# Turning attention values with shifted identities in SBUF, postponing the first adjacency pieces, and ending layer 0's norm on ScalarE

## The chip, the cores and the metric

The kernel runs on one core of one Trainium2 chip. The core has five engines with a queue of instructions each: TensorE (PE; its weight loads are shown apart as PEld), VectorE (DVE), ScalarE (ACT), GpSimd (POOL) and SyncE (SP), which only issues DMAs. Sixteen DMA engines move data between DRAM, where all inputs lie, and SBUF, the on-chip memory that the engines read; TensorE writes to PSUM, from where DVE or ACT copy results away. The metric is the device time of one execution in microseconds, given as the median of repeated runs.

## The reference

Four layers over 3327 nodes with 128 features, each followed by a residual and a layer norm. Layer 0 is attention with a weighted adjacency matrix as edge bias; layers 1 to 3 are graph convolutions with the same matrix:

```python
q = (x @ Wq.T).reshape(d, n, h)      # d = 128, n = 3327, h = 8
k = (x @ Wk.T).reshape(d, n, h)
v = (x @ Wv.T).reshape(d, n, h)
a = softmax(einsum('dnh,dmh->dnm', q, k) * scale + adj + adj, axis=2)
out = einsum('dnm,dmh->dnh', a, v).reshape(n, h * d)
x0 = layernorm(x + out @ Wo.T)
# layer 1: normalised (adj + I) @ (x @ W.T + b); layer 2: adj/deg and adj.T/deg;  layer 3: [x, adj @ x] @ W.T + b
```

The reshape is a plain reinterpretation of memory: the 3327 rows of 1024 projected numbers are read again as 128 "heads" of 3327 rows with 8 numbers. With one slot being 8 numbers, a row of the projection holds 128 slots, and head d begins at slot 3327 d, in the middle of a row. So a head's rows are not aligned to rows of x, and head d + 1 is shifted against head d.

## The kernel before

**Setup** (the block of pools at lines 241 to 378). x is read in seven super-blocks of 512 rows (`u`, the last one half as long), transposed on PE into `xT` (L267) and multiplied by the weights, which are transposed so that a column is (h, j) (`load_by_h`, L166). The products (`products`, L281) go through two PSUM buffers `pp`. Three things happen with them:

- For queries and keys (L324 to L336) ACT writes a rounded copy `hi` (L330), DVE the rest `lo` (L331) and the largest magnitude of `hi` (L333), and the POOL queue stores both to DRAM tensors of slots `q_s` and `k_s` (L275). `hi` and `lo` have two buffers each.
- For values (L284 to L288) the product is copied into `pv` and stored by the POOL queue to `vT_s` in DRAM (L275). `values_turned(g)` then reads sixteen heads of it back, shifted as the flat layout has it (`vt`, L300, on the SP queue), transposes 26 tiles of 128 tokens on PE (L312), copies them to `vo` (L317), and stores `vo` from the ACT queue to `v_img` (L320), the layout that attention reads.
- For the first super-block of 512 rows of the adjacency matrix (u = 0), thirteen "pieces" of 512 x 256 are loaded (`piece_load`, L185), transposed in 32 x 32 blocks, reduced for row maxima, row sums and column sums (`piece_work`, L200 to L216), and stored transposed to `adjT_s` in 16 small DMAs each on the POOL queue (`piece_store`, L224). Row maxima go to `lead_s` (L237).

Outside of `manual_schedule` a scheduler orders each engine's queue from the dependencies and its own estimates; the order is fixed when the kernel is compiled.

**Attention** (`attention`, from L381; the order is written out by hand). 28 blocks are worked through: seven chunks of 476 queries times four ranges of keys (`KBS`). In each block 32 groups of four heads are computed: scores on PE (L575), exponentials on ACT (L583; a few on DVE, L539 to L546), weighted values on PE (L600). DMAs of queries and keys are issued two groups ahead, the POOL copies values into padded tiles (L481). In every eighth group one more piece of the adjacency matrix is handled in the background (`background`, `background_work`); the list `pieces` has u = 1 to 6, 78 pieces, so it is used up after 624 of the 896 groups.

**After attention** (from L943). For each of 26 tiles of 128 nodes `divide` loads the attention output `o` (L1054, SP queue), takes a reciprocal on DVE (`rec`, L1056), multiplies on POOL (`on`, L1058); PE transposes (L1066), multiplies by Wo (L1075); DVE adds x (L1078) and `norm` ends with L1008 on DVE, `(h - mean) * rstd`. This is stage 0. Then come four passes over the stored adjacency matrix, in which PE works without gaps.

Of the kernel before, what the change touches and what calls it, by code (L numbers as in the profile page):

```python
# [19 lines left out]
P = 128  # L20
# [30 lines left out]
def kernel(ctx: ExitStack, tc: tile.TileContext, x, adj, wq, wk, wv, wo,  # L51
# [31 lines left out]
    def tokens(t):  # L83
        return P - 1 if t == T - 1 else P
# [31 lines left out]
    vT_s = scratch.tile([H, SLOTS], F32, name="vT_s")  # L116
# [78 lines left out]
    def piece_work(pool, u, c, ai):  # L195

        nj = PIECE // 32
        w = min(PIECE, N - c * PIECE)
        at = pool.tile([P, nj, 4, 32], F32, name="at")
        nc.vector.transpose(at.rearrange("p j t b -> p t j b"), ai.rearrange("p t (j a) -> p t j a", a=32))  # L200
        yield at
        if c == 0:
            maxima[u] = pool.tile([P, 4, NPC], F32, name="pmax")
            sums[u] = pool.tile([P, 4, NPC], F32, name="psum")
        nc.vector.tensor_reduce(maxima[u][:, :, c], ai[:, :, 0:w], AX.X, ALU.max)
        yield at
        nc.vector.tensor_reduce(sums[u][:, :, c], ai[:, :, 0:w], AX.X, ALU.add)
        yield at
        part = csum[:, c * nj:(c + 1) * nj]
        if u == 0:  # L210
            nc.vector.tensor_reduce(part, at.rearrange("p j t b -> p j (t b)"), AX.X, ALU.add)
        else:
            cs = pool.tile([P, nj], F32, name="cs")
            nc.vector.tensor_reduce(cs, at.rearrange("p j t b -> p j (t b)"), AX.X, ALU.add)
            nc.vector.tensor_tensor(part, part, cs, ALU.add)
        yield at  # L216

    def piece_store(pool, u, c, at):
# [8 lines left out]
        if c == NPC - 1:  # L227
            nc.vector.tensor_reduce(rsum[:, u, :], sums[u], AX.X, ALU.add)
            top = pool.tile([P, 4], F32, name="rtop")
            nc.vector.tensor_reduce(top, maxima[u], AX.X, ALU.max)  # L230
            hi = pool.tile([P, 4], F32R, name="rhi")
            nc.vector.tensor_copy(hi, top)
            lo = pool.tile([P, 4], F32R, name="rlo")
            nc.vector.tensor_tensor(lo, top, hi.bitcast(F32), ALU.subtract)
            for row, sb in enumerate((hi, lo)):
                for i in range(4):
                    nc.gpsimd.dma_start(out=flat_ap(lead_s[u], row * SUPER + i * P, [[1, 32], [32, 4]]),  # L237
                                        in_=sb[32 * i:32 * i + 32, :].bitcast(F32))


    with tc.tile_pool(name="pw", bufs=1) as pw, tc.tile_pool(name="pa", bufs=2) as pa, \
            tc.tile_pool(name="pe", bufs=2) as pe, \
# [10 lines left out]
        wvT = load_by_h(pw, ppw, wv, "wvT")  # L253
        for u in range(NU):
# [10 lines left out]
            ps = pps.tile([P, 4, P], F32, tag="ps", name="xtr")  # L265
            for r in range(R):
                nc.tensor.transpose(ps[:, r, :], xr[:, r, :], ident)  # L267
            copy(u, xT[:, u, 0:R, :], ps[:, 0:R, :])
# [14 lines left out]

        for u in range(NU):  # L284
            pv = pa.tile([P, H, 4, D], F32, tag="hi", name="pv")
            for r in range(spread(u)[1]):
                copy(u + r, pv[:, :, r, :], products(u, r, wvT))
            store_slots(nc.gpsimd, vT_s, 0, u, pv)  # L288

        wqT = load_by_h(pw, ppw, wq, "wqT")  # L290
        wkT = load_by_h(pw, ppw, wk, "wkT")
        top_q = pw.tile([P, NU, 4], F32, name="top_q")
        top_k = pw.tile([P, NU, 4], F32, name="top_k")
        nc.gpsimd.memset(top_q, 0.0)
        nc.gpsimd.memset(top_k, 0.0)

        def values_turned(g):

            vt = pa.tile([P, N], F32, name="vt")
            nc.sync.dma_start(out=vt, in_=flat_ap(vT_s, g * 16 * N, [[N, 16], [SLOTS, H], [1, N]]))  # L300
            vo = pa.tile([P, 4 * T * 32], F32, name="vo")

            nc.gpsimd.memset(vo[96:P, :], 0.0)
            i = 0
            for k0, nt in KBS:
                vb = vo[:, 4 * 32 * k0:4 * 32 * (k0 + nt)].rearrange("p (g s c) -> p s g c", g=4, c=32)
                for s0 in range(0, nt, 4):
                    ns = min(4, nt - s0)
                    ps = pps.tile([P, 4, P], F32, tag="ps", name="vtr")
                    for j in range(ns):  # L310
                        m = tokens(k0 + s0 + j)
                        nc.tensor.transpose(ps[:m, j, :], vt[:, (k0 + s0 + j) * P:(k0 + s0 + j) * P + m], ident)  # L312
                    m = tokens(k0 + s0 + ns - 1)
                    for b, e in ([(0, ns)] if m == P else [(0, ns - 1), (ns - 1, ns)]):
                        if b < e:
                            mm = tokens(k0 + s0 + e - 1)
                            copy(i, vb[:mm, s0 + b:s0 + e], ps[:mm, b:e, :].rearrange("p s (g c) -> p s g c", g=4))  # L317
                    i += 1
                w = nt * 32
                nc.scalar.dma_start(  # L320
                    out=flat_ap(v_img, k0 * HD + g * 4 * w, [[T * HD, P], [w, 4], [1, w]]),
                    in_=vo[:, 4 * 32 * k0:4 * 32 * (k0 + nt)].rearrange("p (g c) -> p g c", g=4))

        for u in range(NU):  # L324
            for w, s, top, f in ((wqT, q_s, top_q, SCALE / 2), (wkT, k_s, top_k, 1.0)):
                hi = pa.tile([P, H, 4, D], F32R, tag="hi", name="hi")
                lo = pa.tile([P, H, 4, D], F32R, tag="lo", name="lo")
                for r in range(spread(u)[1]):
                    pp = products(u, r, w)
                    nc.scalar.activation(hi[:, :, r, :], pp, AF.Copy, scale=f)  # L330
                    nc.vector.scalar_tensor_tensor(lo[:, :, r, :], pp, f, hi[:, :, r, :].bitcast(F32),  # L331
                                                   ALU.mult, ALU.subtract)
                    nc.vector.tensor_reduce(top[:, u, r:r + 1], hi[:, :, r, :].bitcast(F32), AX.XY, ALU.max,  # L333
                                            apply_absolute_value=True)
                store_slots(nc.gpsimd, s, 0, u, hi.bitcast(F32))
                store_slots(nc.gpsimd, s, H, u, lo.bitcast(F32))  # L336
            values_turned(u)
            for c in range(2 * u, min(2 * u + 2, NPC)):
                for at in piece_work(pe, 0, c, piece_load(pe, 0, c)):
                    pass  # L340
                piece_store(pe, 0, c, at)
        for g in range(NU, D // 16):
            values_turned(g)
# [16 lines left out]
        nc.vector.tensor_reduce(top[:, 0:1], top_q, AX.XY, ALU.max)  # L360
        nc.vector.tensor_reduce(top[:, 1:2], top_k, AX.XY, ALU.max)
# [19 lines left out]
    def attention():  # L381
        with tc.tile_pool(name="acc", bufs=1) as accp, tc.tile_pool(name="kq", bufs=3) as kq, \
# [106 lines left out]
            pieces = [(u, c) for u in range(1, NU) for c in range(NPC)]  # L489
# [510 lines left out]
    def norm(n, h, dst):  # L1000
# [7 lines left out]
        nc.vector.tensor_scalar(dst, h, mv[:n, 0:1], rstd[:n, :], ALU.subtract, ALU.mult)  # L1008
# [60 lines left out]
    def outputs(t):  # L1069
# [9 lines left out]
        norm(n, h[:n, :], xs[0][:n, t, :])  # L1079
# [125 lines left out]
```

## Time and profile before

| what | us |
|---|---|
| median of 3 runs (lowest to highest) | 11061.58 (11059.64 to 11064.08) |
| the profiled execution's own time | 11066.37 |
| its span | 11064.6 |
| setup, to the first exponential on ACT | 439.4 |
| a block of attention, 7 key tiles / 6 key tiles | 372.2 / 328.8 |
| stage 0, from the first load of `o` to the first L1041 | 10283.1 to 10403.2 |

Over the whole span PE is busy for 95%, ACT for 89%, DVE for 66% and POOL for 14%. That is an average: attention takes 89% of the span and has almost no gaps, while in the setup no engine is near its limit. Times below are microseconds from the start of the span; a line such as L331 is a line of the kernel before. In a table of windows, each row gives for a stretch of time how long each engine was busy (and how many instructions it ran), then the granted clock of TensorE as a share of full speed, the mean busy share of the 16 DMA engines, and the rate in GB/s.

### The profile page before, as it was taken

The page shows a single profiled execution, that of the slowest core. Times are in us where ns is not written, and L with a number is a line of the kernel's source. Part 1 is how long each engine was busy: PE and PEld are TensorE (multiplying, and loading weights), DVE is VectorE, ACT ScalarE, POOL GpSimd, SP SyncE. Part 2 cuts the span into 40 slices and gives each one's busy share as a digit, 9 for nine tenths or more (in the row PEclk, how much of TensorE's full clock was granted, in tenths as well). Part 3 has the DMA queues.
Part 4 walks back from the last instruction along what each step waited for, and adds up shares of the span by engine and source line. Part 5 has one row for each costly group of instructions (what it writes and reads, how often), then busy time and mean ns, then how long its engine had stood idle before and what let it go on. Part 6 is the DMA issues. An engine that isn't in the chain of part 4 may idle for free. (4 is left out here: it accounts for less than half of the span.)

```text
span 11064.6 us, 201055 instructions
## 1 busy us (share of the span) xinstructions
PE 10517.7 (95%) x76607; PEld 4050.4 (37%) x76607; DVE 7309.3 (66%) x8368; ACT 9830.9 (89%) x10746; POOL 1588.4 (14%) x2765
## 2 busy tenths in 40 slices
PE   6599999999999999999999999999999999999899
PEld 2233333333333333333333333333333333333779
DVE  6466777667776677766777666776667766676512
ACT  2499999999999999999999999999999999999300
POOL 3311112111121111211112110110000100001200
PEclk8799999999999999999999999999999999999999
DMA  8888888888888888888888888888888888788686
GB/s 282 199 124 126 128 130 136 123 126 127 133 133 123 128 126 133 134 124 128 126 130 136 122 122 121 124 122 119 115 116 116 120 119 116 115 110 119 199 283 241
DMA packets 987019, 1536.52 MB, mean 139 GB/s; under 512 B 202881, under 2 KB 796611, under 8 KB 971723
## 3 DMA queue, kind: packets, MB, share of 16 engines
q1 hardware_dynamic: 897430, 1378.57, 78.1%
q0 software_dynamic: 83296, 130.51, 4.7%
q8 instruction: 621, 10.17, 0.5%
q10 hardware_dynamic: 5332, 14.49, 0.4%
q14 instruction: 340, 2.79, 0.1%
HBM read 1378.68 MB, written 143.98 MB: 138 GB/s over the span
## 5 line engine op out<-in xcount | busy, mean ns | idle before, releaser
L583 ACT ACTIVATE e<-sc 128x952 f32<-128x952 f32 (+1 forms) x10304 | 9643.7, 1067 | 215.4 <-PE sc L575 182.6
L600 PE MATMUL o<-e,v_pad 128*32 128x476 f32 (+1 forms) x46592 | 5637.7, 573 | 40.0 <-DVE acc L613 37.1
L575 PE MATMUL sc<-qt,kt 64*128 64x476 f32 x23296 | 4474.6, 438 | 240.6 <-ACT e L583 167.0
L575 PEld LDWEIGHTS sc<-qt,kt 64*128 64x128 f32 x23296 | 2186.2, 184 | 4552.6 <-ACT e L583 4258.1
L600 PEld LDWEIGHTS o<-e,v_pad 128*32 128x32 f32 (+1 forms) x46592 | 1037.5, 108 | 1942.6 <-issue 1901.8
L539 DVE TENSOR_SCALAR ey<-sc 128x952 f32<-128x952 f32 x448 | 515.1, 1150 | 1670.0 <-PE sc L575 1669.6
L481 POOL COPY v_pad<-vs 128x192 f32<-128x192 f32 (+1 forms) x896 | 427.9, 503 | 8286.2 <-DMA vs<-v_img 6658.8
L545 DVE SCALAR_TENSOR_TENSOR e<-e,ey 128x952 f32<-128x952 f32 x1344 | 1546.1, 1150 | 43.2
L465 DVE TENSOR_SCALAR qt<-qt 32x1428 fp32r<-32x1428 f32 x896 | 800.6, 893 | 417.6 <-DMA qt<-q_s 331.9
L467 DVE CAST qt<-qt 64x1904 fp32r<-64x1904 f32 x896 | 1035.4, 1156 | 30.5
L224 POOL DMA_DIRECT2D adjT_s<-at x1352 | 781.4, 585 | 262.7 <-DMA adjT_s<-at 114.3
L541 DVE SCALAR_TENSOR_TENSOR ey<-et,ey 128x952 f32<-128x952 f32 x448 | 516.0, 1152 | 15.5
L545 DVE SCALAR_TENSOR_TENSOR e<-e,et 128x952 f32<-128x952 f32 x448 | 514.8, 1149 | 12.5
L545 DVE SCALAR_TENSOR_TENSOR e<-ey 128x952 f32<-128x952 f32 x448 | 514.5, 1149 | 0.0
L1041 PE MATMUL bank<-y,eT 128*128 128x128 f32 (+1 forms) x4056 | 473.9, 276 | 0.8 <-DVE h L1163 0.4
L1041 PEld LDWEIGHTS bank<-y,eT 128*128 128x128 f32 (+1 forms) x4056 | 465.3, 192 | 6.1 <-DVE h L1163 0.6
L613 DVE TENSOR_TENSOR acc<-o,acc 128x476 f32<-128x476 f32 x231 | 150.4, 651 | 441.5 <-PE o L600 440.6
L466 DVE TENSOR_SCALAR qt<-qt 32x476 fp32r<-32x476 f32 x896 | 356.1, 397 | 4.8 <-DMA qt<-lead_s 3.7
L1006 ACT ACTIVATE rstd<-mv,eps 128x1 f32<-128x1 f32 x104 | 30.6, 294 | 316.3 <-DVE mv L1004 316.3
L540 DVE TENSOR_SCALAR et<-ey 128x952 f32<-128x952 f32 x448 | 296.9, 663 | 15.4
L542 DVE TENSOR_SCALAR et<-et 128x952 int32<-128x952 int32 x448 | 295.3, 659 | 15.4
L330 ACT ACTIVATE hi<-pp 128x1024 fp32r<-128x1024 f32 x52 | 52.8, 1025 | 180.4 <-PE pp L281 155.3
(149 smaller groups left out, 2460.1 us busy)
## 6 DMA issues: line engine op xcount, KB each, us to landing
kt<-k_s SPq DMA_DIRECT2D x5320, 96.0 KB
kt<-k_s SPq DMA_DIRECT2D x1764, 128.0 KB
eT<-adjT_s SPq DMA_DIRECT2D x78, 1664.0 KB
qt<-q_s SPq DMA_DIRECT2D x896, 119.0 KB
qt<-q_s SPq DMA_DIRECT2D x1792, 59.5 KB
vs<-v_img SPq DMA_DIRECT2D x224, 224.0 KB
adjT_s<-at POOLq DMA_DIRECT2D x1352, 32.0 KB, 5.3
vs<-v_img SPq DMA_DIRECT2D x224, 192.0 KB
```

The lines of the kernel that those rows point to most:

```text
L224: nc.gpsimd.dma_start(out=flat_ap(adjT_s, (t * P + 32 * q) * NP + c * PIECE, [[NP, 32], [P, ns], [1, P]]), in_=at[32 * i:32 * i + 32].rear ...
L465: return [(0.9, None, lambda: nc.vector.tensor_scalar(qt[32:64, 1:], qf[0:32, 0:GROUP - 1], -1.0, None, ALU.mult)), (0.4, None, lambda: nc ...
L466: (0.4, None, lambda: nc.vector.tensor_scalar(qt[32:64, 0], before, -1.0, None, ALU.mult)),
L467: (1.2, None, lambda: nc.vector.tensor_copy(qt[64:128], qf[0:64]))]
L481: nc.gpsimd.tensor_copy(vp[:, 32:32 + nt * GROUP * 32].rearrange("p (x c) -> p x c", c=32)[:, :, 0:H], vs.rearrange("p (x c) -> p x c", c=H))
L539: nc.vector.tensor_scalar(y, x, -58 * math.log(2.0), 2 / math.log(2.0), ALU.max, ALU.mult)
L541: vec.append((1.2, of, lambda: nc.vector.scalar_tensor_tensor(y, t, ROUND, y, ALU.subtract, ALU.subtract)))
L545: vec.append((1.2, of, lambda i=i, a=a: nc.vector.scalar_tensor_tensor(e, e if i else y, a, t if i == len(POLY) - 1 else y, ALU.add, ALU.m ...
L575: nc.tensor.matmul(s[:, i, 0:CW], lhsT=kt[64 * rg:64 * rg + 64, k, pos * P:(pos + 1) * P], rhs=qt[64 * rg:64 * rg + 64, k, :], start=False ...
L583: nc.scalar.activation(e[:, 0:n, :], s[:, 0:n, 0:CW], AF.Exp, scale=2.0)
L600: nc.tensor.matmul(o[32 * j:32 * j + 32, 0:CW], lhsT=values[b, g][:m, c:c + 32], rhs=es[b, g * GROUP + j, r][:m, :], start=(r == 0 and u = ...
L1041: nc.tensor.matmul(ps[:n, 0:D], lhsT=e[:m, s, :n], rhs=y[:m, s, col:col + D], start=(s == 0), stop=(s == T - 1))
```

## The change

Three edits.

1. Values. `vT_s`, its stores and the loads of `vt` are gone. The setup's loop runs over u once: queries and keys of u (`split`, which now takes one reduction over all rows of `hi` in place of one for each product), then `values_projected(u)`: `wvT` is the stationary operand and a natural-order copy of x's transpose, `xN`, streams, so that the 512 rows of x lie along the free axis of `vp[u]` for each h. Then `values_turned(d)`, for two heads at once: a matrix of zeros with an identity in its middle (`turn`, 128 x 384) is read at an offset, so that a multiplication by it shifts the 128 slots of a row by r; the part that wraps into the next row is a second matmul into the same PSUM region. One copy moves the pair of heads to `vo`, and after sixteen heads `vo` is stored to `v_img` as before.
2. Adjacency. The thirteen pieces of u = 0 are no longer in the setup; they stand at the end of the background list (91 pieces). The row maxima of these 512 rows, which the start of attention needs, come from four loads of whole rows (`ar`, SP queue) with one reduction each.
3. Norm. In stage 0 `norm` computes `off = -mean * rstd` on DVE (128 x 1) and ACT does the large operation, `Identity(h * rstd + off)`.

```diff
+    def store_tops(pool, u, top, n):
+        hi = pool.tile([P, 4], F32R, name="rhi")
+        nc.vector.tensor_copy(hi, top)
+        lo = pool.tile([P, 4], F32R, name="rlo")
+        nc.vector.tensor_tensor(lo, top, hi.bitcast(F32), ALU.subtract)
+        for row, sb in enumerate((hi, lo)):
+            for i in range(P // n):
+                nc.gpsimd.dma_start(out=flat_ap(lead_s[u], row * SUPER + i * P, [[1, n], [n, 4]]),
+                                    in_=sb[n * i:n * i + n, :].bitcast(F32))
...
-            copy(u, xT[:, u, 0:R, :], ps[:, 0:R, :])
+            nc.vector.tensor_copy(xT[:, u, 0:R, :], ps[:, 0:R, :])
+            nc.scalar.copy(xN[:, base:base + R * P].rearrange("c (p r) -> c r p", r=R), ps[:, 0:R, :])
+            if u == 0:
+                wkT = load_by_h(pw, ppw, wk, "wkT")
+                wvT = load_by_h(pw, ppw, wv, "wvT")
...
+        turn = pw.tile([P, 3 * P], F32, name="turn")
+        nc.gpsimd.memset(turn, 0.0)
+        nc.gpsimd.tensor_copy(turn[:, P:2 * P], ident)
+        vp, vo = {}, {}
+
+        def values_projected(u):
+            n = spread(u)[1] * P
+            vp[u] = pa.tile([P, H, SUPER], F32, name="vp")
+            for h in range(H):
+                ps = pps.tile([P, SUPER], F32, tag="ps", bufs=3, name="pv")
+                nc.tensor.matmul(ps[:, 0:n], lhsT=wvT[:, h * D:(h + 1) * D], rhs=xN[:, u * SUPER:u * SUPER + n],
+                                 start=True, stop=True)
+                copy(h, vp[u][:, h, 0:n], ps[:, 0:n])
+
+        def values_turned(d):
+            g, i = d // 16, d % 16
+            if i == 0:
+                vo[g] = pa.tile([P, 4, T, 32], F32, tag="wide", name="vo")
+            ps = pps.tile([P, 2, H, T], F32, tag="ps", bufs=3, name="vtr")
+            for k in range(2):
+                q, r = (d + k) * N // D, (d + k) * N % D
+                for wrap in range(2 if r else 1):
+                    at = q + wrap
+                    while at < q + wrap + T:
+                        u = at // SUPER
+                        n = min(q + wrap + T, (u + 1) * SUPER) - at
+                        s = at - q - wrap
+                        first = (0 if wrap else P) + r
+                        nc.tensor.matmul(ps[:, k, :, s:s + n], lhsT=turn[:, first:first + P],
+                                         rhs=vp[u][:, :, at - u * SUPER:at - u * SUPER + n],
+                                         start=(k == 0 and wrap == 0 and s == 0), stop=True,
+                                         skip_group_check=True)
+                        at += n
+            copy(d // 2, vo[g][:, i // 4, :, i % 4 * H:(i % 4 + 2) * H].rearrange("p s (k h) -> p k h s", k=2), ps)
+            if i == 14:
+                for k0, nt in KBS:
+                    w = nt * 32
+                    nc.scalar.dma_start(out=flat_ap(v_img, k0 * HD + g * 4 * w, [[T * HD, P], [w, 4], [1, w]]),
+                                        in_=vo[g][:, :, k0:k0 + nt, :].rearrange("p g s c -> p g (s c)"))
...
+            nc.vector.tensor_reduce(top[:, u:u + 1], hi[:, :, 0:R, :].bitcast(F32), AX.XYZ, ALU.max,
+                                    apply_absolute_value=True)
...
         for u in range(NU):
...
+            split(u, wqT, q_s, top_q, SCALE / 2)
+            split(u, wkT, k_s, top_k, 1.0)
+            values_projected(u)
+            last = u * SUPER + spread(u)[1] * P
+            while d < D and (d + 1) * N // D + T < last:
+                values_turned(d)
+                d += 2
+            if 1 <= u <= 4:
+                ar = pa.tile([P, NP], F32, tag="wide", name="ar")
+                load_rows(nc.sync, ar[:, 0:N], adj, u - 1)
+                nc.vector.tensor_reduce(tops[:, u - 1:u], ar[:, 0:N], AX.X, ALU.max)
+            if u == 4:
+                store_tops(pw, 0, tops, P)
...
-            pieces = [(u, c) for u in range(1, NU) for c in range(NPC)]
+            pieces = [(u, c) for u in [*range(1, NU), 0] for c in range(NPC)]
...
+        if on_scalar:
+            off = small.tile([P, 1], F32, name="off")
+            nc.vector.tensor_scalar(off[:n, :], mv[:n, 0:1], rstd[:n, :], -1.0, ALU.mult, ALU.mult)
+            nc.scalar.activation(dst, h, AF.Identity, bias=off[:n, :], scale=rstd[:n, :])
+        else:
+            nc.vector.tensor_scalar(dst, h, mv[:n, 0:1], rstd[:n, :], ALU.subtract, ALU.mult)
```

## The prediction

> **What bounds the kernel now.** I read the setup first in windows of 10 us, because the change works there. One cycle of the loop over u, as it repeats from about 160 to 360:
>
> ```profile
> 220.00:230.00 10.00, 6.59 (x24) 3.03 (x22) 9.17 (x10) 2.18 (x4) 5.66 (x6) 0.99 1.02 331
> 230.00:240.00 10.00, 0.00 (x0) 0.00 (x0) 0.87 (x1) 1.94 (x2) 1.61 (x4) 0.50 1.02 356
> 240.00:250.00 10.00, 0.00 (x0) 0.00 (x0) 4.60 (x4) 0.00 (x0) 1.08 (x2) 0.50 1.04 413
> 250.00:260.00 10.00, 5.61 (x7) 2.52 (x8) 5.35 (x5) 1.02 (x1) 5.71 (x11) 0.50 0.44 154
> 260.00:270.00 10.00, 7.94 (x27) 3.56 (x27) 9.45 (x10) 3.92 (x5) 9.35 (x17) 0.98 0.40 113
> 270.00:280.00 10.00, 7.34 (x28) 3.48 (x25) 9.21 (x10) 2.66 (x5) 4.91 (x4) 1.00 1.01 341
> ```
>
> The columns after the length are PE, PEld, DVE, ACT, POOL, granted clock, DMA share, GB/s. For 30 us the DMA engines are full (1.01 to 1.04) and PE does nothing; for 20 us the engines compute and the DMA share is 0.40 to 0.44. Transfers and computation take turns, about 50 us a cycle. The groups of the setup say why:
>
> ```profile
> L224 POOL DMA_DIRECT2D adjT_s<-at x208 | 110.9, 541 | 103.2 <-DMA q_s<-lo 36.5 <-DMA k_s<-lo 29.7 <-DMA k_s<-hi 24.9
> L331 DVE SCALAR_TENSOR_TENSOR lo<-pp,hi 128x1024 fp32r<-128x1024 f32 x52 | 62.7, 1219 | 32.3 <-ACT hi L330 28.8 <-DMA q_s<-lo 3.3
> L330 ACT ACTIVATE hi<-pp 128x1024 fp32r<-128x1024 f32 x52 | 52.8, 1025 | 180.4 <-PE pp L281 155.3 <-DMA q_s<-hi 25.1
> L205 DVE TENSOR_REDUCE pmax<-ai 128x4 f32<-128x1024 f32 x12 | 14.5, 1211 | 42.8 <-DMA ai<-in_adj_dram 42.8
> L312 PE MATMUL vtr<-ident,vt 128*128 128x128 f32 x200 | 37.4, 332 | 43.3 <-ACT vo L142 34.0 <-DVE vo L144 7.1 <-DMA vt<-vT_s 2.0
> ```
>
> 208 issues of 0.54 us stand in POOL's queue among the stores of `hi` and `lo`; while they issue, the large stores behind them have not begun. While the large stores run, `hi` cannot be refilled, and DVE waits 42.8 us for `ai` with L331 queued behind. Attention is another matter: blocks of equal key range, from windows cut at their starts, first two with background pieces, 6 key tiles with and without, then the first 7-tile block of three chunks, two with and one without:
>
> ```profile
> 5736.30:6065.10 328.80, 320.89 (x2329) 106.82 (x2329) 250.65 (x272) 319.67 (x369) 76.95 (x132) 1.00 0.87 135
> 8540.60:8869.40 328.80, 320.82 (x2328) 106.70 (x2328) 231.16 (x252) 319.63 (x369) 38.72 (x68) 1.00 0.84 122
> ```
> ```profile
> 4658.80:5035.00 376.20, 361.74 (x2708) 128.95 (x2708) 251.49 (x276) 369.47 (x369) 62.66 (x113) 1.00 0.89 127
> 6065.10:6437.30 372.20, 360.00 (x2708) 128.47 (x2708) 253.44 (x284) 368.96 (x369) 55.89 (x92) 1.00 0.86 124
> 7467.10:7839.30 372.20, 360.18 (x2708) 128.47 (x2708) 231.04 (x252) 368.99 (x369) 21.19 (x40) 1.00 0.83 117
> ```
>
> ACT and PE set the length; DVE has over 70 us to spare. Last, stage 0 in the timeline, an L1008 alone and one beside POOL's multiplication:
>
> ```profile
> 10309.61 0.35 DVE L1008 TENSOR_SCALAR x<-h,mv,rstd 128x128 f32<-128x128 f32 x1
> ...
> 10325.35 2.51 DVE L1008 TENSOR_SCALAR x<-h,mv,rstd 128x128 f32<-128x128 f32 x1
> 10325.42 2.35 POOL L1058 TENSOR_TENSOR on<-o,rec 128x1024 f32<-128x1024 f32 x1 [1.81 <-DVE rstd L1007]
> ```
>
> L1008 ends 0.08 us after POOL does: 0.35 becomes 2.51 us, in 18 of 26 steps.
>
> **Setup, the work.** I measure its end by the first full block: block 1 starts at 817.3 (first L568) and a 7-tile block takes 372.2, so setup and start of attention cost 445.1.
>
> *DMA.* The packet records before 445 sum to 362.7 us of 16 engines. Sorted by queue and size they give: five stores of slots (4096 B, q, k twice, v once) 184.0, so `vT_s` 36.8; `vt` loads (1024 of 13308 B) 48.4; `adjT_s` stores (2048 B) 26.9; `ai` loads (1024 and 1020 B) 24.9. These 137.0 go. The four `ar` loads are 512 rows of 13308 B, half of the `vt` packets: 24.2 come. 249.9 us remain; for one u: stores (184.0 - 36.8)/6.5 = 22.6, `v_img` 41.7/6.5 = 6.4, `ar` 3.7, x and small ones about 1: 34. (Six and a half super-blocks.)
>
> *PE.* A float32 matmul is two instructions (104 of L281 for 52). At full clock ten of 512 columns take 4.56 us (0.44 with their spacing); of 128 columns, L1041, 176 in 20 us (0.114). A line through both gives 0.174 at 199 columns. Queries and keys: 32 x 0.44 = 14.1 per u. `values_projected`: 16 x 0.44 = 7.0. `values_turned`: counting q, r and wraps for all 128 heads gives 267 matmuls with 199 columns on average, 42 in a full u: 84 x 0.174 = 14.6. Sum 35.7 per u, where 52 matmuls of L281 for values and 208 transposes were before. That is more work than before; it replaces DRAM traffic.
>
> *DVE.* Per u: 8 L331, 9.8; two reductions of 4096 (L333 has 1.21 for 1024, 0.18 for 28, so 4.4), 8.8; half of the copies, 4 x 0.69 and 5 x 0.58 (by L144, 0.685 for 512), 5.7; `ar`, 3.6 in four of them. 28 in all; ACT 14. POOL loses 110.9 us of L224, 7.4 of `vT_s` issues and 23.0 of L303; its queue keeps stores of q and k and the lead rows.
>
> **Setup, the time.** PE (35.7) and DMA (34) are now nearly equal, and run together, as PE has values to work on while stores drain. 35.7 is the lower end. The upper end of PE's term is the present loop's clock: windows give 0.74 for 90 to 365, so 35.7/0.74 = 48.2. I take 43 per u, a little above the middle: the two long reductions stand before the next L331 and before a copy of `values_projected`, each holds PSUM buffers about 4 us, and each `ar` reduction waits on its load in DVE's queue with the next u's L331 behind it (the `ai` waits were 56.0/8 = 7 us each). `ar` shares two buffers with `vo`, so SP waits there for a `v_img` store; behind it on SP stand only later loads. Start 13 us (first L281 at 9, `wq` first as `wv` was, plus a second copy of xT), end 30.4 (last `v_img` issue at 414.7 to 445.1, unchanged). 13 + 6.5 x 43 + 30.4 = 323 against 445.1: **-122**.
>
> A rule of the Trainium skill speaks against this sum. "TensorE: Matmul & The Clock Gate", Part 1, has the clock at half after an idle window of about 3.4 us and at full only after as long a busy one. The trace agrees in kind (0.50 in 230 to 260, 1.00 from 270). By the row of windows 43 per u follows; if gaps kept PE at half clock, the term would be 71.4 and the setup 507, 62 slower. I go by the row, since PE's work per u is now about as long as DMA's and it no longer stands still in the 30 us of a drain.
>
> **Background.** Thirteen pieces move past every earlier piece to groups 624 to 727, blocks 19 to 22: 4 SP loads, 16 POOL issues (0.585 each) and five DVE operations of up to 1.2 us per piece, 13 x 5 = 65 us on DVE. Cover: DVE's idle 98 to 141 us a block (328.8 - 231.2, 372.2 - 231.0). 6-tile blocks show no price (328.8 and 328.8); the first 7-tile block of a chunk 0 to 4 (372.2 and 376.2). Without the cover, 65 us. **+2**, ends 0 and 4 (four blocks are touched, one of them the first 7-tile block of a chunk). They are stored long before layer 1 reads them.
>
> **Norm.** From 10321 to 10391, 17 steps take 4.12 us each. PE alone would need 3.56 (L1066 at 10317.90 and at 10321.46, no gap between). Seventeen steps x 0.56 = 9.5 if DVE is freed; ACT gains 0.39 per step (L1084) and has 26 of 70 us busy. But `off` stands where L1008 stood, is also a TENSOR_SCALAR from SBUF to SBUF, and if it waits for POOL too, nothing is gained. The skill's "SBUF — State Buffer", Who interferes with whom, says a copy or tensor_scalar in a two-port mode locks the port pair that POOL shares; whether one element counts no row here shows. By the row, L1008 itself, 0; by the small L1007 between them (0.12), 9.5. **-5**, the middle, as both ends are below what matters. The pass after it is PE's and keeps what is gained.
>
> **Sum.** -122 - 5 + 2 = -125. The profiled execution took 11066.4 (span 11064.6 and 1.8 around it), so 10941; its distance to the median is -4.8: 11061.6 - 125 = **10937**. Its own range, 37 to 48 per u: 10895 to 10970.
>
> **Rivals.** *Transfers are the only bound*: everything hides under 34 per u; 13 + 221 + 30 = 264, -181 and -3: 10878. For it: windows of 1.02 today; against it: equal PE work, DVE's reductions. *A wait takes the place of the one removed*: `ar` loads, the shared buffers of `vo` and the 4.4 us reductions put 50 or more into each u: 13 + 325 + 30 = 368, -77 and -3: 10982. For it: the waits on `ai`; against it: only four such loads. *Slower*: TensorE stays cold in the loop, 71.4 per u, +62 - 3: 11121; it decides from 61.8 per u on, a mean clock of 0.58; against it, 0.90 in the first 90 us, where PE had work. *The change doesn't do what it says*: the fixed queue order puts values after the stores again, and cycles stay between 58.4 and 65 per u: within 0.2%.
>
> **Chances.** Forecast 0.57, transfers 0.15, waits 0.22, unchanged 0.03, slower 0.03. A measurement of this kernel tells 0.2%, 22 us, from no change. Faster 0.94, same 0.03, slower 0.03. The range takes in the transfers case and most of the waits: 10872 to 11000, leaving about 0.06 below and 0.12 above.
>
> **What would show it.** First exponential near 317; no alternation of full and 0.4 DMA windows; clock above 0.85 in the loop; `vtr` matmuls near 0.17 us spacing; POOL with about 45 issues there. 6-tile blocks at 329 in 19 to 22. Stage 0: `off` at 0.15 (step 3.6) or at 2.4 us (step 4.1). The prediction is wrong if matmuls on `turn` run at half clock, or if DVE waits for `ar` by tens of us.

## The result, and the profile after

| | median of runs, us | lowest to highest |
|---|---|---|
| before | 11060.61 | 11056.98 to 11064.08 |
| changed | 10948.72 | 10942.83 to 10954.31 |

The ratio is 0.9899, with a 95% interval from 0.9882 to 0.9916: 112 us less, where 125 were forecast. The forecast of 10937 is 12 us too low and its range (10872 to 11000) holds the time. That the total came out near is partly luck, since the terms of the sum missed in opposite directions, as the next sections show.

The code moved, so the lines have new numbers: the copy `hi` is L345 (L330 before), `lo` L346 (L331), the multiplication by shifted identities L327 (the transposes were L312), the stores of `vo` L336 (L320), the copies L141 and L143, the exponential L611 (L583), in stage 0 `rec` L1089, `on` L1091, `off` L1038 and the large step on ACT L1039.

I cut the profiled executions at the same places as in the prediction: the setup is the start of block 1, the first full block, less 372.2 us; attention runs from that start to the last exponential; stage 0 up to the first multiplication with `eT`; then the rest. So the four parts add up to the span less 372.2.

| us | setup | attention | stage 0 | rest | span |
|---|---|---|---|---|---|
| before | 445.1 | 9456.5 | 129.4 | 661.4 | 11064.6 |
| changed | 341.4 | 9466.9 | 114.4 | 657.2 | 10952.1 |
| difference | -103.7 | +10.4 | -15.0 | -4.2 | -112.5 |

**Setup.** First the windows of the kernel before and of the changed one over the loop (length; busy time and instructions of PE, PEld, DVE, ACT, POOL; granted clock; DMA share; GB/s), then some of 10 us.

```profile
20.00:415.00 395.00, 205.06 (x539) 96.47 (x537) 214.33 (x218) 79.88 (x116) 164.02 (x259) 0.74 0.83 278
```
```profile
20.00:308.00 288.00, 246.82 (x877) 159.93 (x875) 178.34 (x149) 96.31 (x125) 32.12 (x40) 0.95 0.78 263
...
130.00:140.00 10.00, 10.00 (x57) 9.93 (x56) 5.82 (x5) 1.78 (x2) 0.00 (x0) 1.00 1.01 371
220.00:230.00 10.00, 5.60 (x22) 5.16 (x22) 0.85 (x1) 2.43 (x3) 0.00 (x0) 0.83 1.02 355
230.00:240.00 10.00, 10.00 (x36) 6.11 (x35) 3.75 (x5) 3.77 (x5) 0.00 (x0) 1.00 0.54 173
270.00:280.00 10.00, 5.99 (x23) 3.77 (x21) 2.02 (x4) 0.00 (x0) 0.00 (x0) 1.00 0.71 206
```

PE was busy for 52% of the loop and is now for 86% (246.8 of 288), at a clock of 0.95 in place of 0.74; POOL has 40 instructions and not 259. At 130 PE and the DMA engines are both full, as the forecast had it. But at 220 the DMA engines are full and PE has 4.4 us of gaps, and at 270 to 280 neither is full, DVE stands for 8 us and ACT runs nothing at all. The groups of the setup and the timeline (start, length, engine, line, operands, and the idle time before with what ended it) say what is behind this:

```profile
L327 PE MATMUL vtr<-vp,turn 128*128 128x208 f32 (+5 forms) x534 | 99.7, 346 | 10.0 <-ACT vo L141 5.9 <-DVE vp L143 3.1 <-ACT vp L141 0.8
L289 PE MATMUL pp<-wkT,xT 128*128 128x512 f32 x104 | 57.7, 694 | 11.6 <-DVE lo L346 10.7 <-DVE rhi L220 0.5 <-ACT wkT L141 0.4
L345 ACT ACTIVATE hi<-pp 128x1024 fp32r<-128x1024 f32 x52 | 52.7, 1024 | 90.6 <-PE pp L289 75.0 <-issue 12.5 <-DMA v_img<-vo 3.2
L141 ACT COPY vo<-vtr 128x416 f32<-128x416 f32 x32 | 27.7, 883 | 74.7 <-PE vtr L327 52.5 <-DVE vo L143 12.4 <-issue 9.8
L143 DVE COPY vo<-vtr 128x416 f32<-128x416 f32 x32 | 27.2, 875 | 47.1 <-PE vtr L327 47.1
L368 DVE TENSOR_REDUCE tops<-ar 128x1 f32<-128x3327 f32 x4 | 14.5, 3619 | 9.9 <-DMA ar<-in_adj_dram 9.9
```
```profile
215.15 9.52 ACTq L336 DMA_DIRECT2D v_img<-vo  x4
...
224.92 1.56 ACT L141 COPY vo<-vtr 128x416 f32<-128x416 f32 x2 [9.79 <-issue]
225.82 6.27 PEld L327 LDWEIGHTS vtr<-vp,turn 128*128 128x128 f32 x26 [4.73 <-ACT vo L141]
225.82 6.43 PE L327 MATMUL vtr<-vp,turn 128*128 128x208 f32 x25 [4.40 <-ACT vo L141]
```

Four issues of `v_img` stores hold ACT's queue for 9.5 us; ACT is idle for 9.8 us before the copy behind them, and PE, which needs the PSUM buffer that this copy frees, stands for 4.4 us. The same happens at 269, where four issues take 12.2 us. All 32 issues of the kernel before and of the changed one (duration: least, median, most):

```profile
L320 ACTq DMA_DIRECT2D v_img<-vo x32: 325/326/784, 71.0 to 414.7; - x32
```
```profile
L336 ACTq DMA_DIRECT2D v_img<-vo x32: 366/1296/6189, 66.4 to 306.6; - x32
```

They sum to 11.2 us before and 45.8 us after. The 366 ns are those of a first issue of four. In all eight groups of four the first took 0.37 to 0.40 us, the later ones 0.5 to 6.2; in the kernel before, the issues came one at a time, mostly 1.6 us or more apart. The stores carry the same bytes, but `vo` is now kept by groups of four heads, so that a run of bytes in it is 896 or 768 B and no longer 3584 or 3072 B: the packets of ACT's DMA queue rose from 5332 to 17620.

**Blocks that hold the thirteen moved pieces** (19 and 20), as windows of the changed kernel:

```profile
7035.30:7367.00 331.70, 321.93 (x2328) 106.89 (x2328) 251.52 (x276) 320.05 (x369) 77.92 (x126) 0.99 0.84 130
7367.04:7745.04 378.00, 362.79 (x2709) 129.70 (x2709) 252.04 (x273) 369.37 (x369) 58.44 (x104) 0.99 0.89 127
```

Blocks 19 to 22 last 1412.8 us together, against 1402.2 before.

**Stage 0**, from the timeline. POOL's multiplication begins at 10217.83; `off` begins 1.11 us into it:

```profile
10217.83 2.35 POOL L1091 TENSOR_TENSOR on<-o,rec 128x1024 f32<-128x1024 f32 x1 [2.11 <-PE bank L1099]
```
```profile
10218.74 0.16 DVE L1035 RECIPROCAL rstd<-rstd 128x1 f32<-128x1 f32 x1 [0.36 <-ACT rstd L1034]
10218.94 0.21 DVE L1038 TENSOR_SCALAR off<-mv,rstd 128x1 f32<-128x1 f32 x1
10219.26 0.95 DVE L1089 RECIPROCAL rec<-o 128x128 f32<-128x128 f32 x1
```

It takes 0.21 us, while an L1008 of the kernel before that began 1.13 us into such a multiplication took 1.30 us and ended 0.09 us after it:

```profile
10311.95 2.34 POOL L1058 TENSOR_TENSOR on<-o,rec 128x1024 f32<-128x1024 f32 x1 [3.73 <-DVE rec L1056]
```
```profile
10313.08 1.30 DVE L1008 TENSOR_SCALAR x<-h,mv,rstd 128x128 f32<-128x128 f32 x1
```

All 26 `off` take 212 to 216 ns. Seven begin inside a multiplication, three of them with over 0.3 us of it to go; 16 have one begin 0.07 us after their own start, as the L1008 of 2.51 us in the prediction had, and end 2.2 us before it does. So `off` is not held. The 25 steps from one normalised tile to the next took 101.5 us before and take 85.7 us now.

### The profile page after: what moved, and what is told of

Its sections match the earlier page's. It is cut to its first block, busy times and chain, and to the rows that moved or that the text cites. A ratio compares the mean times of both kernels' runs of the same rounds, so it can differ in the third digit from the quotient of the medians.

```text
span 10952.1 us, 201583 instructions
## 1 busy us (share of the span) xinstructions
PE 10557.4 (96%) x76941; PEld 4117.7 (38%) x76941; DVE 7291.7 (67%) x8351; ACT 9867.2 (90%) x10783; POOL 1585.4 (14%) x2742
## 5 line engine op out<-in xcount | busy, mean ns | idle before, releaser
L611 ACT ACTIVATE e<-sc 128x952 f32<-128x952 f32 (+1 forms) x10304 | 9644.5, 1067 | 227.8 <-PE sc L603 219.9
L1034 ACT ACTIVATE rstd<-mv,eps 128x1 f32<-128x1 f32 x104 | 30.4, 292 | 265.1 <-DVE mv L1032 265.1
L648 POOL DMA_DIRECT2D o_s<-acc x308 | 191.5, 626 | 35.8 <-DVE acc L641 22.4
```

The lines of the kernel that those rows point to most:

```text
L611: nc.scalar.activation(e[:, 0:n, :], s[:, 0:n, 0:CW], AF.Exp, scale=2.0)
```

## Experiments

The three groups of rows were measured on three chips. In each group "before" is the kernel before on that chip, and the ratio is to it. The parts are those of one profiled execution each.

| run | us, median | ratio (95%) | setup | attention | stage 0 | rest |
|---|---|---|---|---|---|---|
| before | 11063.19 | | | | | |
| e1_norm_dve | 10961.41 | 0.9907 (0.9890 to 0.9924) | 338.6 | 9465.6 | 128.7 | 657.3 |
| e2_norm_psum | 11046.04 | 0.9985 (0.9979 to 0.9992) | 438.0 | 9463.0 | 116.2 | 661.4 |
| e3_store_sp | 10946.87 | 0.9894 (0.9878 to 0.9911) | 326.7 | 9469.5 | 114.1 | 663.5 |
| e4_no_u0 | 10950.71 | 0.9899 (0.9882 to 0.9915) | 338.5 | 9458.5 | 114.3 | 660.0 |
| before | 11069.14 | | | | | |
| e5_pe_more | 10992.38 | 0.9934 (0.9917 to 0.9950) | 376.1 | 9461.9 | 115.3 | 657.3 |
| e6_dma_more | 11001.33 | 0.9939 (0.9922 to 0.9956) | 389.4 | 9465.3 | 114.6 | 657.3 |
| e7_adj_only | 10996.93 | 0.9935 (0.9918 to 0.9951) | 377.0 | 9462.7 | 129.5 | 657.3 |
| e8_val_only | 10964.62 | 0.9905 (0.9889 to 0.9922) | 354.7 | 9474.4 | 113.7 | 657.3 |
| before | 11058.32 | | | | | |
| e9_after | 10951.98 | 0.9904 (0.9887 to 0.9920) | 337.0 | 9461.8 | 114.4 | 657.2 |
| e10_store_sp | 10943.80 | 0.9894 (0.9878 to 0.9911) | 325.7 | 9465.8 | 115.0 | 663.5 |
| e11_best | 10924.77 | 0.9876 (0.9860 to 0.9893) | 328.1 | 9447.4 | 117.3 | 663.5 |
| e12_shift | 10931.90 | 0.9885 (0.9868 to 0.9901) | 338.9 | 9445.0 | 115.1 | 657.2 |

### The norm

`e1_norm_dve` undoes the third edit in the changed kernel:

```diff
-        norm(n, h[:n, :], xs[0][:n, t, :], True)
+        norm(n, h[:n, :], xs[0][:n, t, :])
```

> The changed kernel with the norm of stage 0 ended on DVE again, the other two parts kept. Theory (the port that DVE shares with POOL): the big operation takes 2.51 us again beside POOL's multiplication, a step of stage 0 goes from 3.5 back to 4.1 us, the stretch from the last exponential to the first gather matmul from 114 back to 129 us; the time is 15 to 19 us above the changed kernel (10949), near 10965. Rival (the shortening of stage 0 comes from the earlier arrival of o or of the queue order, not from the norm): stage 0 stays at 114 us and the time at 10949.

`e2_norm_psum` leaves the kernel before as it is, large operation on DVE, but keeps its input in PSUM:

```diff
-        h = work.tile([P, D], F32, name="h0")
+        h = ps[:, 0:D]
```

> The kernel before with one edit: in stage 0 the sum h stays in PSUM, so that the norm's last operation on DVE reads PSUM and writes SBUF; DVE does as much work as before, ACT no more. Theory (a shared port, not too much work on DVE): the operation takes about 0.35 us also beside POOL, steps go to about 3.5 us, and the time falls by 10 to 19 us against the kernel before, to about 11045. Rival (DVE has too much work and only moving it to ACT helps): no change, 11061.

Stage 0 is 128.7 us with the large operation on DVE from SBUF, and 113.7 to 117.3 us in the runs that have it on ACT, 116.2 with it on DVE from PSUM. The time of e1 rose less than the 15 to 19 us that were expected, by 12.7 (10961.41 against 10948.72, on different chips). The group of this operation in e1 from 10213 to 10300, and the same line of e2 (duration: least, median, most):

```profile
L1041 DVE TENSOR_SCALAR x<-h,mv,rstd 128x128 f32<-128x128 f32 x21 | 43.9, 2088 | 0.8
```
```profile
L1008 DVE TENSOR_SCALAR x<-bank,mv,rstd x26: 409/410/413, 10306.1 to 10393.5; 128x128 f32<-128x128 f32 x25, 127x128 f32<-127x128 f32 x1
```

From PSUM the same operation takes 0.41 us in every one of 26 cases, 22 of them overlapping POOL's multiplication. So it isn't DVE's work that cost the time but its waiting for POOL from SBUF to SBUF, and a change of one tile's place cures it as the move to ACT does: e2 alone is 17 us faster than the kernel before (0.9985, 0.9979 to 0.9992), of which stage 0 shows 13.

### What bounds the setup

Two experiments add work that nobody reads. `e5_pe_more` adds four multiplications of 128 columns to each pair of heads, 512 instructions in all, 58 us by the prediction's 0.114 us for one:

```diff
+            more = ppw.tile([P, P], F32, tag="w_ps", name="more")
+            for _ in range(4):
+                nc.tensor.matmul(more, lhsT=turn[:, P:2 * P], rhs=turn[:, P:2 * P], start=True, stop=True)
```

> The changed kernel with four matmuls of 128 columns more for each pair of turned heads, into a PSUM bank that nobody reads; by the spacing of such matmuls (0.114 us an instruction, two each) 64 x 8 x 0.114 = 58 us of TensorE work in the setup. Theory (TensorE now bounds the setup): the setup grows by 45 to 58 us, time near 11000. Rival (transfers bound it): TensorE has slack in the loop, below 15 us.

`e6_dma_more` stores `vo` a second time, from SP's queue, to a tensor that is not read (some 40 us of the 16 engines, as much as `v_img`):

```diff
+    v_two = scratch.tile([P, T * HD], F32, name="v_two")
...
+                    nc.sync.dma_start(out=flat_ap(v_two, k0 * HD + g * 4 * w, [[T * HD, P], [w, 4], [1, w]]),
+                                        in_=vo[g][:, :, k0:k0 + nt, :].rearrange("p g s c -> p g (s c)"))
```

> The changed kernel with a second store of the turned values, 13.6 MB, to a DRAM tensor that nobody reads, from the SP queue; by the packet records of the changed kernel this is 42 us of the 16 DMA engines. Theory (TensorE bounds the setup, DMA share 0.74 in it): less than 15 us more. Rival (transfers bound it): 30 to 42 us more, time near 10985.

The setup rose by 34.7 us with the added multiplications (376.1 against 341.4) and by 48 with the added stores (389.4); against the other executions with the changed kernel's setup (337.0 to 338.9 in e1, e4, e9 and e12) it is up to 4 us more. The first lies between its theory and its rival, the second above both. The windows of e5, and of e6 with a row of its waits (sum, times, longest):

```profile
20.00:338.00 318.00, 296.05 (x1381) 214.34 (x1380) 178.30 (x146) 97.42 (x121) 31.77 (x40) 0.97 0.68 238
```
```profile
20.00:350.00 330.00, 251.96 (x876) 163.12 (x874) 178.15 (x149) 95.85 (x124) 32.18 (x40) 0.89 0.81 266
```
```profile
DVE tops L371 <- DMA ar<-in_adj_dram: 39.8, 4, 12.6
```

Neither theory of a single bound stands. If transfers alone set the end, e5 would have cost nothing; if PE alone did, e6 would have cost nothing. In e5 PE fills 93% of the loop; its busy time up to the last `v_img` issue grew by 48 us (259.8 to 307.5), and 35 of these show, the others went into PE's former gaps. In e6 a part of the price comes by way of a wait: `ar` shares its two buffers with `vo`, so with slower stores of `vo` its loads begin late, DVE waits 39.8 us for them (9.9 in the changed kernel) with `lo` queued behind, and the clock falls to 0.89. So e6 shows that the setup is sensitive to the drain of `vo`, not the worth of a transfer by itself.

### The parts of the setup

`e7_adj_only` takes the kernel before and gives it only the second edit (row maxima from `ar`, here with two buffers of its own, the pieces of u = 0 at the end of the background list). `e8_val_only` takes the changed kernel and puts the pieces of u = 0 back. The core of e7's edit, and then of e8's:

```diff
-            for c in range(2 * u, min(2 * u + 2, NPC)):
-                for at in piece_work(pe, 0, c, piece_load(pe, 0, c)):
-                    pass
-                piece_store(pe, 0, c, at)
+            if 1 <= u <= 4:
+                ar = pa.tile([P, NP], F32, name="ar")
+                load_rows(nc.sync, ar[:, 0:N], adj, u - 1)
+                nc.vector.tensor_reduce(tops[:, u - 1:u], ar[:, 0:N], AX.X, ALU.max)
...
-            pieces = [(u, c) for u in range(1, NU) for c in range(NPC)]
+            pieces = [(u, c) for u in [*range(1, NU), 0] for c in range(NPC)]
```
```diff
-            if 1 <= u <= 4:
-                ar = pa.tile([P, NP], F32, tag="wide", name="ar")
...
+            for c in range(2 * u, min(2 * u + 2, NPC)):
+                for at in piece_work(pe, 0, c, piece_load(pe, 0, c)):
+                    pass
+                piece_store(pe, 0, c, at)
```

> The kernel before with the adjacency part alone: pieces of the first 512 rows at the end of the background list, row maxima from four loads of whole rows; values still go through DRAM, the norm is as before. Theory (the small stores on the POOL queue kept transfers and computation taking turns): cycles of the loop over u fall from 49 to about 35 us and the setup by 60 to 90 us, with 8 us given back in attention; time near 10995. Rival (the way of the values through DRAM is what costs): 10 to 30 us, time near 11040.

> The changed kernel with the thirteen pieces of the first 512 rows back in the setup, two for each u, and without the row loads; values are turned in SBUF and the norm ends on ScalarE. Theory (both parts are needed, the POOL queue's small stores again stand among the large ones): cycles of about 50 us and a setup of about 390, time near 10993, of which 13 us is the norm. Rival (the values' part alone gives nearly all): setup near 345, time near 10950.

Alone, the adjacency edit takes 68 us off the setup (445.1 to 377.0) and the values edit 90 (to 354.7); together they take 104 to 108, not 158. The theory of e7 held and that of e8 failed: its setup is nearer to the rival's 345 than to the theory's 390. The loops of e7 and of e8:

```profile
20.00:350.00 330.00, 213.53 (x561) 101.33 (x559) 170.62 (x179) 82.57 (x120) 60.66 (x63) 0.79 0.91 307
```
```profile
20.00:300.00 280.00, 242.18 (x876) 159.06 (x875) 212.17 (x194) 96.32 (x125) 124.34 (x215) 0.95 0.85 283
```

The two edits remove the same thing twice: in e8, without the values' trip through DRAM, the 208 issues (POOL has 215 instructions) and the `ai` loads fit beside PE's work, which fills 86% of the loop as in the changed kernel. On top of the values edit, moving the pieces is worth 13 to 18 us of setup in the profiles and no more than the intervals of the ratios can hide (0.9905 for e8; 0.9899 and 0.9904 for the changed kernel).

### The stores of `vo`

One word is changed, so that SP issues the stores:

```diff
-                    nc.scalar.dma_start(out=flat_ap(v_img, k0 * HD + g * 4 * w, [[T * HD, P], [w, 4], [1, w]]),
+                    nc.sync.dma_start(out=flat_ap(v_img, k0 * HD + g * 4 * w, [[T * HD, P], [w, 4], [1, w]]),
```

> The changed kernel with the stores of the turned values issued from the SP queue instead of the ACT queue. Theory (ACT is held up by the issues, 45.8 us of its queue where it was 11.2, and TensorE stands still behind it near 220 and from 275 to 282): the setup ends 8 to 15 us earlier, first exponential near 322 instead of 333.9, time near 10937. Rival (the loop is bound by TensorE's own work and the gaps have other causes): 0 to 3 us, time 10946 to 10949. Second rival (SP's loads of adjacency rows are held up behind the stores): slower by some us.

> The changed kernel once more, as the base of this call. Theory: 10945 to 10952, ratio to the kernel before 0.990; setup to the start of the first full block's worth 338 to 342 us, attention blocks with a surplus of 15 to 22 us over 372.2 and 329.0, falling on the first 7-tile block of chunks and on blocks that hold postponed pieces.

> The stores of vo to v_img issued from SP's queue in place of ACT's, nothing else. Theory (ACT's queue is held by these issues, 46 us of it, and PE's products wait for ACT's copies meanwhile): setup 12 to 15 us shorter than the changed kernel on the same chip, and the time 10 to 15 us lower. Rival (the gain seen in one profile is eaten elsewhere, as the stores and loads on SP now wait for each other): setup shorter by 5 or less, time within 5 us of the changed kernel.

The setup is 326.7 us in e3 and 325.7 in e10, against 337.0 in the changed kernel beside it: -11.3, where e10 expected 12 to 15. Five executions with the changed kernel's setup (that kernel, e1, e4, e9, e12) have 337.0 to 341.4, three with the stores on SP (e3, e10, e11) 325.7 to 328.1. The time fell by 8.2 us (10951.98 to 10943.80), short of the 10 to 15 expected, because the rest of the program became 6.3 us longer (663.5 against 657.2; see the last section); the four times of each overlap (10944.84 to 10956.85, 10939.02 to 10946.38). By its time alone e3, at 10946.87 where 10937 was expected, would speak for its rival; the setup decides. The groups of e10's setup show that the wait is what went:

```profile
L327 PE MATMUL vtr<-vp,turn 128*128 128x208 f32 (+5 forms) x534 | 98.1, 344 | 0.2 <-ACT vp L141 0.2
...
L345 ACT ACTIVATE hi<-pp 128x1024 fp32r<-128x1024 f32 x52 | 53.0, 1023 | 87.0 <-PE pp L289 85.3 <-DVE lo L346 1.7
```

PE's wait before L327 is 0.2 us in place of 10.0, and ACT has no "issue" time before `hi` and `vo`. A rule of the Trainium skill ("DMA: Bandwidth & Descriptors", Issuing engines are not separate DMA queues) says that another issuing engine saves only the sequencer's time, which is usually small beside the transfer. The mechanism is as it says. The size is not small here: 45.8 us of issuing beside 41.9 us that the packets of these stores took of the 16 engines.

### The pieces in the background

`e4_no_u0` leaves the thirteen pieces out:

```diff
-            pieces = [(u, c) for u in [*range(1, NU), 0] for c in range(NPC)]
+            pieces = [(u, c) for u in range(1, NU) for c in range(NPC)]
```

> The changed kernel without the thirteen pieces of the first 512 adjacency rows; this part of the computation is left out, and the gather of the first four tiles reads the tiles 4 to 7 in their place. Theory (the pieces have a price in attention): blocks 19, 20 and 22 go back to about 328.8, 372.2 and 329.1 us, 7 to 11 us less in attention, time near 10939. Rival (the 10 us by which attention was longer in the profiled run are differences between executions): blocks 19 to 22 stay as they were on average, 0 to 3 us less.

Its blocks 19 to 22 take 1402.9 us. Over eight profiled executions with the pieces (the changed kernel, e1, e3, e5, e6, e7, e9, e10) the four blocks take 1406.2 to 1412.8, mean 1409.6; over four without (before, e2, e4, e8) 1402.2 to 1409.0, mean 1404.1. The pieces cost some 5.5 us, with single executions between about nothing and 11. The timed median of e4 (10950.71) shows no gain over the changed kernel's. Attention as a whole lasts 9464.9 us in the mean with the pieces and 9463.1 without: most of the +10.4 between the two profiles of the first table is scatter between executions, and it sits mostly in the first 7-tile block of a chunk, in the kernel before too (373.9, 377.1 and 376.2 in blocks 4, 8 and 12, where later ones take 372.2).

`e12_shift` keeps all pieces but moves each step four groups later in the cycle of eight, away from the first groups of a block; `e11_best` has that and the stores from SP:

```diff
-                if n % PACE == 0 and pieces:
+                if n % PACE == 4 and pieces:
-                if n % PACE == 6 and worked:
+                if n % PACE == 2 and worked:
-                if n % PACE == 3 and loaded:
+                if n % PACE == 7 and loaded:
-                if n % PACE == 5 and turning:
+                if n % PACE == 1 and turning:
```

> The changed kernel with the background steps four groups later and nothing else. Theory: setup as in the changed kernel, attention 8 to 20 us shorter, time 10930 to 10942. Rival: attention and time within 4 us of the changed kernel.

> Stores of vo from SP, and every background step four groups later in its cycle of eight (load in the fifth group, work in the eighth and second, store in the third), so that no step of a piece falls on the first groups of a block, where the edge loads and the output stores are. Theory (the pieces' price is the meeting of their DMAs with the loads at block starts): first 7-tile blocks within 1 us of 372.2, attention 8 to 20 us shorter, in all 20 to 30 us below the changed kernel. Rival (the price comes with the block starts themselves, or with the total of DMA work): surplus the same, only the setup's 12 to 15 are gained.

In e12 the first 7-tile blocks of these chunks (4, 8, 12, 16, 20) take 372.4 to 372.5 us, attention 9445.0, and the time is 20.1 us below the changed kernel beside it (10931.90). Its four blocks 19 to 22 take 1402.1 us, no more than without the pieces. Blocks 19 and 20:

```profile
7021.71:7350.45 328.74, 320.88 (x2329) 106.84 (x2329) 252.15 (x276) 319.72 (x369) 68.45 (x118) 1.00 0.84 131
7350.45:7722.80 372.35, 360.27 (x2709) 128.53 (x2709) 251.32 (x272) 369.14 (x369) 57.71 (x104) 1.00 0.89 129
```

DVE and ACT do the same work as before the shift (252.04 and 369.37 in the changed kernel), but 5.6 us sooner. What met at the start of block 20 is seen on SP's queue, first of the changed kernel, then of e12:

```profile
7377.95 2.27 SPq L184 DMA_DIRECT2D ai<-in_adj_dram  x4
7380.78 0.39 SPq L437 DMA_DIRECT2D e_in<-in_adj_dram  x1
7381.54 0.27 SPq L439 DMA_DIRECT2D e_in<-in_adj_dram  x1
7382.46 2.29 SPq L463 DMA_DIRECT2D qt<-q_s  x3
7385.02 13.87 SPq L470 DMA_DIRECT2D kt<-k_s  x8
7399.18 0.34 SPq L505 DMA_DIRECT2D vs<-v_img  x1
7400.03 1.50 SPq L463 DMA_DIRECT2D qt<-q_s  x3
```
```profile
7359.58 0.40 SPq L437 DMA_DIRECT2D e_in<-in_adj_dram  x1
7360.29 0.27 SPq L439 DMA_DIRECT2D e_in<-in_adj_dram  x1
7364.71 1.14 SPq L463 DMA_DIRECT2D qt<-q_s  x3
7365.89 12.30 SPq L470 DMA_DIRECT2D kt<-k_s  x8
7378.29 0.37 SPq L505 DMA_DIRECT2D vs<-v_img  x1
7378.77 1.20 SPq L463 DMA_DIRECT2D qt<-q_s  x3
```

With the piece's load `ai` ahead of the loads for the next groups, the last `qt` shown is issued 33.0 us after the block's start (7367.04), without it 28.3 (after 7350.45). In the first 48 us DVE waits 12.1 us for `qt` in the one and 5.2 in the other, ACT waits 8.3 and 3.1 us for scores. The shift moved a piece's load, work and stores together, so which of them costs most was not separated; the rows speak for the load.

e11 is the fastest: 10924.77 us, 27.2 below the changed kernel beside it. It is 20 from the shift and 7 from the stores, nearly the sum of e12 and e10 (28.3); here the times with and without the stores on SP do not overlap (10919.99 to 10930.26 in e11, 10930.31 to 10934.03 in e12).

## Why the prediction was right, and where it was not

**Setup (-122; measured -104, and -108 in e9, both from the 445.1 of before).** e2, whose setup is that of the kernel before, has 438.0, so one execution can differ from another by 7 us here, and the gain is 97 to 108. The mechanism held: transfers and PE's work, forecast at 34 and 35.7 us per super-block and so nearly equal, now overlap instead of taking turns. The first exponential came at 333.9 where 317 was named:

```profile
333.92 1.36 ACT L611 ACTIVATE e<-sc 128x1428 f32<-128x1428 f32 x1 [25.72 <-PE sc L603]
```

The step that failed is the term 13 + 6.5 x 43 + 30.4. From the first product at 9.5 to the last `v_img` issue at 306.6 a super-block took 45.7 us and not 43, and the tail 34.8. So the start is 3.5 us shorter, the loop 17.6 longer and the tail 4.4 longer than forecast. The row of this stretch splits the 45.7:

```profile
9.51:306.59 297.08, 256.20 (x903) 164.96 (x902) 182.45 (x156) 101.14 (x130) 32.64 (x41) 0.95 0.77 258
```

PE was busy for 39.4 us per super-block, where 35.7 was summed, and idle for 6.3, where 43 had allowed 7.3. Of the 3.7 more, the clock of 0.95 makes about 1.9 (an estimate: 35.7/0.95 = 37.6), and the transposes of x and of weights, which the sum did not count here, about 1. The idle time holds what the sum put at nothing: the cost of the `v_img` stores was carried over from the kernel before as bytes only; what their issue costs ACT's queue was left out, though the new layout of `vo` stood in the diff. In e10 PE is busy for as long (255.2 us up to the last issue of these stores) and idle for 30.6 us in place of 40.9, and the setup is 11.3 us shorter; it was 14 to 18 us longer than forecast. The reductions and the `ar` waits, for which the 7.3 had stood, thus cost at most 4.7, and this hid a part of both errors. The copies to `vo` too take 0.88 us and not 0.58: 64 of them make 19 us more, shared by two engines that are not full. By how much that counts was not tried. With the stores on SP the setup is within 3 to 5 us of the forecast of 323.

**Clock.** The rule that spoke against the change ("TensorE: Matmul & The Clock Gate", Part 1) hardly came into play: 0.95 in the loop, against 0.74. Taking the row of windows and not the rule was right. The slower rival, which needed a mean clock of 0.58, had nothing for it; where e6 opened gaps, 0.89 was the price.

**Two readings.** In the three rows from 220 to 250, PE did not do nothing for 30 us: it was busy for 6.6 us of the first, and stood for 23. And 37 us per super-block gives 10897 by the terms of the sum, not 10895. Neither moves the forecast.

**Background (+2, ends 0 and 4; measured about +5.5).** The cover that was named, DVE's idle time, is there. The step "6-tile blocks show no price" looked at DVE alone: of a step that is moved its DMAs count too, and a piece's load in SP's queue at the start of a block is what e12 points to.

**Norm (-5, ends 0 and -9.5; measured -15.0).** Two things failed. The middle was taken because no row shows whether `off` waits for POOL; it doesn't. A rule of the Trainium skill speaks against a wait: "VectorE: DVE Perf Modes", Mode 2×_2P, lets a single-source operation use both port pairs only if source and destination lie in SBUF and have an outermost dimension longer than one that can be split (even, or odd and equal in both). `off` has one element per partition and so, as I read the rule, no such dimension, and e2's source lies in PSUM. The 0.21 and 0.41 us beside POOL agree with the rule. And the end of -9.5 counted 17 steps between two marks; over all 25 steps 101.5 us became 85.7, a mean of 3.43 per step, below the 3.56 read from a single one.

**The rivals.** "Transfers are the only bound" (10878) fell with e5. "A wait takes the place of the one removed" (10982) is true in kind and small in size: not `ar` (9.9 us of waits) but the issues in ACT's queue. e6 shows how near the `ar` wait was. "The change doesn't do what it says" fell with the first window: though full and half-full DMA windows still alternate (a share of 1.02 and 0.54 at 220 and 230), which the prediction had ruled out, PE works through most of them.

So +18 on the setup, -10 on the norm, +3.5 on the pieces and -4.2 at the very end, which no step had, sum to +7; with the scatter of attention between the two profiled executions it is the 12 us by which the forecast was low.

## What to carry to other kernels

When a tile's layout changes, price its DMAs anew by the length of the runs of bytes: on a compute engine's queue several issues in a row can hold that engine (9.5 and 12.2 us here), and one word moves them to a queue that has time. Two edits that cure the same alternation of transfers and computation don't add: e7 and e8 took 68 and 90 us alone and 104 together. Where background work is free on the average, look at what its DMAs meet at the few places where the foreground's own loads crowd; a shift by half a period was worth 20 us here and needed no less work.

## What the runs showed of the hardware that was not expected

An issue of a store from ACT took 0.33 us in the median with 128 packets of 3584 or 3072 B and 1.3 us, up to 6.2, with 512 packets of 896 or 768 B. The number of packets alone doesn't do it: the first of each group of four has 512 too and took 0.37 to 0.40 us. The two longest groups of four (9.5 us at 215, 12.2 at 269) stand beside stretches with full DMA engines (a share of 1.02 from 220 to 230, 1.22 from 260 to 270); whether it is the packets of the issues just before or the full engines that hold an issue was not separated. From SP's queue the same 32 issues took 36.6 us.

The end of the program has a length of its own that goes with the build. In e9 and in e10 the last issues of the output are these:

```profile
10938.64 1.10 POOL L92 DMA_DIRECT2D out_dram<-res  x2 [5.23 <-DVE res L1041]
```
```profile
10931.88 1.10 POOL L92 DMA_DIRECT2D out_dram<-res  x2 [5.23 <-DVE res L1041]
```

From their end to the end of the span it is 3.0 us in e9 (span 10942.7) and 9.1 us in e10 (10942.1); the kernel before has 7.1. Every profile with the stores on SP (e3, e10, e11) has 663.5 for the rest, while the changed kernel, e1, e5 to e9 and e12 have 657.2 or 657.3, with the same passes before; the kernel before and e2 have 661.4, e4 660.0. The cause stays open; it is 4 of the 112 us gained, and it hides 6 of the 11 us that e10 gains in the setup.
